# Layer-norm scales computed as a power on GpSimd, and two pieces of a first stage moved later

## The chip, the cores and the metric

The kernel runs on one core of one Trainium2 chip. A core has a matrix engine (TensorE, "PE"; its weight loads are listed as "PEld"), a vector engine (VectorE, "DVE"), a scalar engine with tabulated functions (ScalarE, "ACT"), a general engine (GpSimd, "POOL") and a queue engine that issues transfers (SyncE, "SP"). Matrix results land in eight banks of 128 x 512 float32. The metric is the device time of one execution in microseconds; a lower number is better.

## What is computed

Input `x` is 4 batches x 2048 rows x 256 columns, float32. Two layers follow each other, each a normalization whose result feeds two branches that are added to `x`:

```
def _layernorm(x, axis=-1, eps=1e-05):
    m = jnp.mean(x, axis=axis, keepdims=True)
    v = jnp.var(x, axis=axis, keepdims=True)
    return (x - m) / jnp.sqrt(v + eps)
...
    x = L0_attn_x
    xn = _layernorm(x, axis=-1)
    x = x + _L0_attn_ref(xn, ...) + _L0_ffn_ref(xn, ...)
    xn = _layernorm(x, axis=-1)
    x = x + _L1_attn_ref(xn, ...) + _L1_ffn_ref(xn, ...)
    return x
```

In layer 0, `_L0_attn_ref` is a gated linear recurrence along the rows (two 256 x 256 gate products, tanh, exp, a square root, then an associative scan). `_L0_ffn_ref` is attention with 16 heads of width 64, of which the 4 with the largest mean routing score are computed; softmax over all 2048 keys, then an output projection. In layer 1, `_L1_attn_ref` is causal attention with 16 heads of width 16, and `_L1_ffn_ref` a channel mix (mixing with the previous row, a squared ReLU, a sigmoid gate).

## The kernel before, in words

One Python function, `two_layers` (L73), writes all instructions. Batches are done one after the other. Inside a batch, layer 0 comes first and layer 1 second, and the tail of layer 1 is mixed with the head of the next batch. `in_order` (L26) ties the instructions of PE, DVE, ACT and POOL to the order in which the Python code emits them. So each engine works through its own list in that order, and an instruction that waits holds up everything behind it on its engine. The setup ahead of `in_order` is ordered by the tile scheduler. SP has its own list of transfers.

The order is written out by hand with generators. A stretch of work is a generator, each `yield` in it is a place to pause, and `steps(stream, count)` (L64) runs it on to its next pauses.

**The norm.** `Norm` (L243) holds a batch's rows `xt` in 16 tiles of 128 rows. `stats` (L253) puts mean and variance of a tile into `mv` (DVE). `root` (L257) takes Sqrt(variance + eps) on ACT, `inverse` (L261) the reciprocal on DVE; both work in place on `rs`. `rows` (L264) writes (x - mean) * rs into `xn` (DVE, one instruction a tile), and `turn` (L272) transposes four tiles of `xn` on PE and copies them into `xT`. The trace has a table load of ACT (ACT_TABLE_LOAD) ahead of each such Sqrt, and another ahead of the Exp or Tanh that follows it.

The norm of layer 1 is done in quarters of four tiles (`all_blocks`, L570, inside `attention0`). The norm of layer 0 of the next batch is done for all 16 tiles at once, in `prepared` (L994): it runs in the tail of layer 1, and for batch 0 at the very start of the kernel.

**The recurrence.** `recurrence` (L278) is a generator: 16 steps of `gates`, 9 steps of `chain` for the second half of the columns, then two steps of additions (L327: a constant is added to `y`, one 128 x 2048 instruction on DVE for each half `h`), then eight steps (L334 to L336) that each transpose a 128 x 512 block of `y` on PE and add it to `xt` on DVE. 26 of its 35 steps are done before `attention0` is entered, so the 26th, the addition for h = 0, is the last one ahead of it. The rest are its `background`.

**Attention of layer 0.** `attention0` (L562) goes over 4 heads x 8 pairs of row tiles, 32 pairs in all, plus two turns of its loop to drain (n = 0 to 33). A pair has an early tile `a` and a late tile `c`. Each tile needs scores (PE, four banks), four row maxima and their maximum `nm` (DVE, L499 and L503), four exponentials (ACT, L509), 16 transposes of the exponentials (PE, L517), four copies into `pT` (two on DVE, two on ACT, L523). `weigh` (L537) multiplies by the values, one loop turn later; `project` and `add` (L551, L557) follow two turns later. Banks are handed out in a ring of seven by `bank()` (L117), so a product that wants a bank waits until the bank's last content has been read.

In one turn the order is: first place for background, projections and norm (L606 to L608); transposes of the late tile of the pair before; second place (L621 to L623); projection, addition and, in the last eight pairs, `stats`; scores, maxima and exponentials of `a`; at n = 0 also the last four steps of `values0` (`rest_of_values`, L634); third place for the norm (L635); scores and exponentials of `c` and the weighing of the pair before; transposes of `a`; fourth place for the norm (L657).

A quarter of the norm takes eight such places, thus two pairs: nothing in two, then `root`, then `inverse` and `rows`, then one transposed half in each of two, then nothing in two. The quarters start at n = 27, 29, 31 and 33. At n = 33 there is no pair left to overlap with.

**Layer 1.** `opening1` (L725) sets up its projections. `Heads1.open` (L693) and `values1` (L704) fill tiles on POOL (L696, L711), and `layer1` (L806) uses POOL for masking (L791) and for adding partial results (L804). In the tail `steps(norming, 2)` (L917) runs the next batch's norm two steps at a time.

Of the kernel before, what the change touches and what calls it, by code (L numbers as in the profile page):

```python
# [10 lines left out]
FP = mybir.dt.float32  # L11
BF = mybir.dt.bfloat16
U32 = mybir.dt.uint32
AF = mybir.ActivationFunctionType
ALU = mybir.AluOpType
# [3 lines left out]
P = 128  # L19
QB = 512  # L20
EPS = 1e-5
# [42 lines left out]
def steps(stream, count):  # L64

    for _ in range(count):
        if next(stream, StopIteration) is StopIteration:
            return False
    return True
# [3 lines left out]
def two_layers(ctx: ExitStack, tc: tile.TileContext, x, Wa, Wx, ba, bx, Lam,  # L73
# [4 lines left out]
    PE, ACT, DVE, POOL, SP = nc.tensor, nc.scalar, nc.vector, nc.gpsimd, nc.sync  # L78
# [3 lines left out]
    NT = T // P  # L82
# [7 lines left out]
    const = ctx.enter_context(tc.tile_pool(name="const", bufs=1))  # L90
# [32 lines left out]
    def load_x(b):  # L123
        src = x[b].rearrange("(n p) d -> p n d", p=P)
        both = [half_tile(f"x_{b}_{i}").rearrange("p (n d) -> p n d", d=D) for i in range(2)]
        for q in range(NQ):
            SP.dma_start(rows_of(both, 4 * q, 4), src[:, 4 * q:4 * q + 4, :])
        return both

    def rows_of(both, n, count):  # L130
# [13 lines left out]
    POOL.memset(cmask, 0.0)  # L144
    POOL.affine_select(out=cmask[:, QB - P:QB], in_=cmask[:, QB - P:QB], compare_op=ALU.is_ge, fill=MASKED,
                       base=0, pattern=[[-1, P]], channel_multiplier=1)
    eps_c = const.tile([P, 1], FP, tag="eps", name="eps_c")
    POOL.memset(eps_c, EPS)
    quarter_c = const.tile([P, 1], FP, tag="quarter", name="quarter_c")
    POOL.memset(quarter_c, 0.25)  # L150
    heads_row = const.tile([P, NH], FP, tag="heads_row", name="heads_row")
# [91 lines left out]
    class Norm:  # L243
# [10 lines left out]
            DVE.bn_stats(self.st[:, t, :], rows_of(self.xt, t, 1)[:, 0, :])  # L254
            DVE.bn_aggr(self.mv[:, t, :], self.st[:, t, :])

        def root(self, t, n):  # L257
            ACT.activation(self.rs[:, t:t + n], self.mv[:, t:t + n, 1:2].rearrange("p n o -> p (n o)"),
                           AF.Sqrt, bias=eps_c)

        def inverse(self, t, n):  # L261
            DVE.reciprocal(self.rs[:, t:t + n], self.rs[:, t:t + n])

        def rows(self, q, i0, i1):  # L264
            if i0 == 0:
# [182 lines left out]
    def queries0(b, k, xT, ch, bank):  # L448

        qs = [half_tile(f"q0_{b}_{k + i}") for i in range(2)]  # L450

        def stream():
            for q in range(NQ):
                blk = slice(q * QB, (q + 1) * QB)
                ps = bank()
                for c in range(2):
                    PE.matmul(ps, lhsT=ch.wq[k // 2][:, c, :], rhs=xT[c][:, blk], start=(c == 0), stop=(c == 1))  # L457
                ACT.activation(qs[0][:, blk], ps, AF.Identity, bias=ch.bias_q[:, k // 2:k // 2 + 1])
                for i in range(2):
                    SP.dma_start(qs[1][i * DH:(i + 1) * DH, blk], qs[0][(1 - i) * DH:(2 - i) * DH, blk])  # L460
                yield
        return qs, stream()

    def keys0(b, k, xT, ch, bank):

        kT = c4.tile([P, HT], FP, tag="k0", name=f"k0_{b}_{k}", bufs=2)

        def stream():
            for j in range(NJ):
                ps = bank()  # L470
                for c in range(2):
                    for i in range(2):
                        k0 = i * HT + j * QB
                        PE.matmul(ps[i * DH:(i + 1) * DH, :], lhsT=ch.wk[k][:, c, :], rhs=xT[c][:, k0:k0 + QB],  # L474
                                  start=(c == 0), stop=(c == 1))
                ACT.activation(kT[:, j * QB:(j + 1) * QB], ps, AF.Identity, bias=ch.bias[:, 1, k:k + 1])
                yield
        return kT, stream()
# [83 lines left out]
    def attention0(b, xT, xt, ch, recurring, first, v, rest_of_values, norm, opening):  # L562


        NP = NT // 2
        qk, following = first, None
        background, projecting, norming = recurring, iter(()), iter(())
        older, before = None, None

        def all_blocks():  # L570


            for q in range(NQ):
                yield
                yield
                norm.root(4 * q, 4)
                yield
                norm.inverse(4 * q, 4)
                norm.rows(q, 0, 2)
                norm.rows(q, 2, 4)  # L580
                yield
                for c in range(2):
                    norm.turn(q, c, ACT.copy)
                    yield
                yield
                yield

        for n in range(NA * NP + 2):
            k, i = divmod(n, NP)
            if i == 0 and 0 < k < NA:  # L590
                steps(projecting, 100)
                qk = following
            new = Pair0(b, k, i, *qk, v, xt) if k < NA else None
            a, c = new.tiles if new else (None, None)
            if i == NP - 3 and k + 1 < NA:
                if k % 2:
                    qs, querying = queries0(b, k + 1, xT, ch, bank)
                else:
                    qs, querying = qk[0], iter(())
                kT, keying = keys0(b, k + 1, xT, ch, bank)  # L600
                following = qs, kT
                projecting = concat(querying, keying)
            if n == (NA - 1) * NP + 3:
                norming = all_blocks()

            steps(background, 1)  # L606
            steps(projecting, 1)
            steps(norming, 1)  # L608
            if n >= NA * NP:
                steps(opening, (2, 2)[n - NA * NP])  # L610
            if before:
                late = before.tiles[1]
                late.turn(1)
                late.turn(0)
                late.keep(1, 0, DVE.tensor_copy)
                late.keep(0, 0, DVE.tensor_copy)
                late.keep(0, 1, ACT.copy)
                late.keep(1, 1, ACT.copy)
                for tile_ in before.tiles:
                    tile_.share()  # L620
            steps(background, 1)  # L621
            steps(projecting, 1)
            steps(norming, 1)  # L623
            if older:
                older.project()
                older.add()
                if n - 2 >= (NA - 1) * NP:
                    for t in range(2):
                        norm.stats(2 * (n - 2 - (NA - 1) * NP) + t)
            if new:  # L630
                a.scores(0)
                a.scores(1)
                a.exponentials((0, 1))
                steps(rest_of_values, 4)  # L634
            steps(norming, 1)  # L635
            if new:
                c.scores(1)
            if n >= NA * NP:
                steps(opening, 1)
            if before:  # L640
                before.weigh(0)
            if new:
                c.scores(0)
                c.exponentials((1, 0))
            if before:
                before.weigh(1)
            if new:
                a.turn(1)
                a.turn(0)
                a.keep(1, 0, DVE.tensor_copy)  # L650
                a.keep(0, 0, DVE.tensor_copy)
                a.keep(1, 1, ACT.copy)
            if before:
                before.weighed()
            if new:
                a.keep(0, 1, ACT.copy)
            steps(norming, 1)  # L657
            older, before = before, new
        steps(background, 100)
        for _ in range(8):  # L660
            steps(norming, 1)
            steps(opening, 1)
        steps(norming, 100)
# [330 lines left out]
    def prepared(b, ready):  # L994

        xt = load_x(b)
        norm = Norm(xt, f"0_{b}", own_bank)
        ch = Chosen()
        ready.append((xt, norm.xT, ch))

        def go():
            for t in range(0, NT, 2):
                norm.stats(t)
                norm.stats(t + 1)
                yield
            norm.root(0, NT)
            yield
            norm.inverse(0, NT)
            for q in range(NQ):
                norm.rows(q, 0, 2)  # L1010
                yield
                norm.rows(q, 2, 4)
                yield
                yield
                for c in range(2):
                    norm.turn(q, c, DVE.tensor_copy)
                    yield
        return go(), choose(b, norm.xT, ch)
# [3 lines left out]
    with in_order(tc):  # L1022
# [3 lines left out]
        for b in range(B):  # L1026
# [20 lines left out]
            x1, norm = xt, Norm(xt, f"1_{b}", bank)  # L1047
# [36 lines left out]
```

## Time and profile before

| what | value |
|---|---|
| median of 3 runs (lowest, highest) | 4306.98 us (4306.27, 4307.82) |
| the profiled execution's own time | 4301.88 us |
| span of its trace | 4300.2 us |
| DVE busy | 3101.0 us (72%) |
| ACT busy | 2809.9 us (65%) |
| POOL busy | 1044.2 us (24%) |
| table loads ahead of a Sqrt of the norms (L258) | 20, 25.7 us |
| table loads ahead of the Exps of layer 0 (L509) | 16, 20.5 us |
| table loads ahead of the Exps of layer 1 (L788) | 7, 9.0 us |
| the norms' Sqrt (L258) | 20, 6.0 us |
| the norms' reciprocal (L262) | 20, 3.7 us |
| recurrence's additions (L327) | 8, 9.9 us |

The profile comes from one execution, recorded instruction by instruction. The span runs from its first to its last instruction; the execution's own time is 1.7 us more. Shares are of the span. A "group" is all instructions of one source line, engine and operation. "Idle before" is the time an engine stood still right before an instruction, and the name behind the arrow is what ended that idle time. An engine can be busy nearly all the time and still lose time in a few places, so the places where the busiest engine stood idle matter more than the shares.

### The profile page before, as it was taken

Reading aid. Unit: us, or ns where it says so; the run is one execution under the profiler, and the core shown is the slowest. Engines: PE = TensorE matmul, PEld = TensorE weight load, DVE = VectorE, ACT = ScalarE, POOL = GpSimd, SP = SyncE. Lnnn points to the kernel's source line nnn. Section 1 sums busy time; section 2 is a strip of 40 time slices with the busy share of each in tenths; the row PEclk is TensorE's granted clock in tenths of the full one; section 3 lists DMA queues with packets and bytes.
Section 4 is the critical chain, followed back from the end, with each engine's and each line's share of the span. In section 5 each row is a group of like instructions: output and inputs, shape, how many; then the busy total and the mean of one; then the engine's idle time right before and its main releaser. Section 6 shows DMA issues by size and latency. Waiting matters only on the chain.

```text
span 4300.2 us, 86329 instructions
## 1 busy us (share of the span) xinstructions
PE 4189.6 (97%) x32994; PEld 2345.5 (55%) x32994; DVE 3101.0 (72%) x7292; ACT 2809.9 (65%) x6388; POOL 1044.2 (24%) x1322
## 2 busy tenths in 40 slices
PE   6999999999999999999999999999999999999999
PEld 3777653334577764333457776433446766643334
DVE  5767678887577767888657775888856777588882
ACT  3666648886566664888656665588765666568884
POOL 0000015544100001554410000255440000036544
PEclk9999999999999999999999999999999999999999
DMA  3000010100100000010000000001000000100000
GB/s 85 1 11 2 6 17 17 18 25 17 26 1 11 1 9 16 17 37 6 19 24 1 11 1 18 6 17 37 7 19 23 1 11 1 21 5 17 16 7 23
DMA packets 70818, 65.79 MB, mean 15 GB/s; under 512 B 37234, under 2 KB 58628, under 8 KB 68868
## 3 DMA queue, kind: packets, MB, share of 16 engines
q1 hardware_dynamic: 66624, 57.19, 6.1%
q8 instruction: 260, 4.26, 0.4%
q10 hardware_dynamic: 3780, 3.07, 0.2%
q14 instruction: 154, 1.26, 0.1%
HBM read 16.70 MB, written 8.39 MB: 6 GB/s over the span
## 4 chain that ended last, share of the span: by engine, by line
PE 89%; DVE 5%; ACT 3%; issue 1%; POOL 1%; DMA 1%; ACTq 0%; SPq 0%; POOLq 0%; DVEq 0%
PE bank L786 15%; PE bank L761 14%; PE bank L797 12%; PE bank L517 10%; PE bank L495 10%; PE bank L542 10%; PE bank L972 4%; PE bank L291 3%; PE bank L688 3%; PE bank L555 2%; DVE mx L767 1%; PE bank L474 1%; PE bank L457 1%; PE bank L717 1%; PE bank L960 1%; ACT p L509 1%
## 5 line engine op out<-in xcount | busy, mean ns | idle before, releaser
L788 ACT ACTIVATE p<-bank 128x512 f32<-128x512 f32 (+3 forms) x2560 | 1183.1, 539 | 378.9 <-PE bank L786 275.1
L761 PE MATMUL bank<-k,q 32*128 32x512 f32 (+3 forms) x5120 | 1180.9, 584 | 2.2
L767 DVE TENSOR_REDUCE mx<-bank 128x1 f32<-128x512 f32 x1536 | 950.9, 683 | 197.2 <-PE bank L761 196.4
L786 PE MATMUL bank<-q,k 32*128 32x512 f32 (+3 forms) x5120 | 1074.0, 556 | 0.0
L509 ACT ACTIVATE p<-bank,nm 128x512 f32<-128x512 f32 x1024 | 690.4, 686 | 566.5 <-DVE nm L503 566.3
L804 POOL TENSOR_TENSOR o<-o,w 128x512 f32<-128x512 f32 (+3 forms) x576 | 627.0, 1088 | 796.0 <-ACT w L803 795.7
L786 PEld LDWEIGHTS bank<-q,k 32*128 32x128 f32 x5120 | 422.0, 184 | 544.6 <-ACT p L788 409.4
L499 DVE TENSOR_REDUCE mx<-bank 128x1 f32<-128x512 f32 x1024 | 645.9, 683 | 91.4 <-PE bank L495 90.6
L797 PE MATMUL bank<-p,v 128*17 128x512 f32 (+3 forms) x5120 | 601.3, 534 | 21.4 <-ACT p L788 14.3
L764 DVE CUSTOM_DVE_ANT_0 bank<-bank,cmask 128x128 f32<-128x128 f32 (+3 forms) x1024 | 473.1, 523 | 171.3 <-PE bank L761 116.4
L523 DVE COPY pT<-bank 128x512 f32<-128x512 f32 x512 | 353.1, 692 | 286.3 <-PE bank L517 267.9
L761 PEld LDWEIGHTS bank<-k,q 32*128 32x128 f32 x5120 | 473.5, 188 | 139.3 <-DVE mx L767 48.9
L542 PEld LDWEIGHTS bank<-pT,v 128*64 128x64 f32 x8192 | 442.0, 137 | 191.0 <-issue 191.0
L495 PE MATMUL bank<-k,q 64*128 64x512 f32 x2048 | 542.2, 609 | 0.9
L517 PE MATMUL bank<-ident,p 128*128 128x128 f32 x4096 | 490.8, 275 | 20.0 <-ACT p L509 19.8
L542 PE MATMUL bank<-pT,v 128*64 128x128 f32 x8192 | 502.8, 276 | 0.0
L517 PEld LDWEIGHTS bank<-ident,p 128*128 128x128 f32 x4096 | 445.1, 141 | 68.7 <-ACT p L509 29.8
L696 POOL MEMSET q<- 128x2048 f32 x16 | 28.9, 1808 | 1803.8 <-PE bank L542 1803.8
L803 ACT COPY w<-bank 128x512 f32<-128x512 f32 (+3 forms) x576 | 304.9, 529 | 107.2 <-PE bank L797 85.5
L523 ACT COPY pT<-bank 128x512 f32<-128x512 f32 x512 | 293.7, 601 | 55.6 <-PE bank L517 53.9
L797 PEld LDWEIGHTS bank<-p,v 128*17 128x17 f32 x5120 | 88.7, 95 | 439.8 <-ACT p L788 237.1
L495 PEld LDWEIGHTS bank<-k,q 64*128 64x128 f32 x2048 | 212.5, 188 | 170.0 <-issue 83.4
(164 smaller groups left out, 3346.7 us busy)
## 6 DMA issues: line engine op xcount, KB each, us to landing
x<-in_L_attn_x_dram SPq DMA_DIRECT2D x20, 512.0 KB
q<-q SPq DMA_DIRECT2D x64, 128.0 KB
vals<-o SPq DMA_DIRECT2D x256, 32.0 KB
out_dram<-x SPq DMA_DIRECT2D x32, 256.0 KB
q<-qp SPq DMA_DIRECT2D x48, 128.0 KB
k<-kp SPq DMA_DIRECT2D x48, 128.0 KB
q<-nmT SPq DMA_DIRECT2D x256, 2.0 KB
q<-qp SPq DMA_DIRECT2D x64, 32.0 KB
```

The source lines that it names most:

```text
L495: PE.matmul(self.s[j][i], lhsT=self.qT[i][half_, self.t * P:(self.t + 1) * P], rhs=self.kT[half_, j * QB:(j + 1) * QB], start=True, stop=True)
L499: DVE.tensor_reduce(self.mx[:, n:n + 1], self.s[j][i], AX.X, ALU.max)
L509: ACT.activation(self.p[j][:, i, :], self.s[j][i], AF.Exp, bias=nm, accum_out=self.sums[:, n:n + 1])
L517: PE.transpose(self.tr[j][i][:, n * P:(n + 1) * P], self.p[j][:, i, n * P:(n + 1) * P], ident)
L523: copy(self.pT[:, n0:n0 + 4, :], self.tr[j][i].rearrange("p (n q) -> p n q", q=P))
L542: PE.matmul(acc[i * DH:(i + 1) * DH, 0:P], lhsT=self.v[h][:, N * j + n, self.k * DH:(self.k + 1) * DH], rhs=tile_.pT[:, 8 * h + N * j + n, ...
L761: PE.matmul(s[:, 0:n], lhsT=self.qT[strip(h), self.qs], rhs=self.kT[strip(h), self.ks], start=True, stop=True)
L767: DVE.tensor_reduce(self.mx[:, h, :], s[:, 0:n], AX.X, ALU.max)
L786: PE.matmul(s[:, c0:QB], lhsT=self.kT[strip(h), self.ks], rhs=self.qT[strip(h), self.q0 + c0:self.q0 + QB], start=True, stop=True)
L788: ACT.activation(p[:, h % 2, c0:QB], s[:, c0:QB], AF.Exp, scale=SC1)
L797: PE.matmul(acc[32 * h:32 * h + DH1 + 1, c0:QB], lhsT=self.v[h], rhs=self.p[h // 2][:, h % 2, c0:QB], start=True, stop=True)
L804: POOL.tensor_tensor(self.o[:, c0:QB], self.o[:, c0:QB], w[:, c0:QB], ALU.add)
```

## The change

Three things are changed.

1. `root` is gone. `inverse` now adds eps on DVE (one instruction) and raises the result to the power -0.5 on POOL, against a constant tile `minus_half` of 128 x 16. In `all_blocks` it is called at the place where `root` was called; the place behind it holds `rows` alone. In `prepared` it also takes the place of `root`.
2. At n = 0 the two `background` steps are left out. The addition for h = 1 then falls on the first place of n = 1, and the eight transposed blocks on n = 1 to 5 (one, two, two, two, one) instead of n = 0 to 4 (one, two, two, two, one).
3. Of the last four steps of `values0`, two stay behind the exponentials of the first `a`, and two go behind the scores and exponentials of the first `c`.

```diff
@@ -144,8 +144,8 @@
     POOL.memset(cmask, 0.0)
     POOL.affine_select(out=cmask[:, QB - P:QB], in_=cmask[:, QB - P:QB], compare_op=ALU.is_ge, fill=MASKED,
                        base=0, pattern=[[-1, P]], channel_multiplier=1)
-    eps_c = const.tile([P, 1], FP, tag="eps", name="eps_c")
-    POOL.memset(eps_c, EPS)
+    minus_half = const.tile([P, NT], FP, tag="minus_half", name="minus_half")
+    POOL.memset(minus_half, -0.5)
     quarter_c = const.tile([P, 1], FP, tag="quarter", name="quarter_c")
     POOL.memset(quarter_c, 0.25)
     heads_row = const.tile([P, NH], FP, tag="heads_row", name="heads_row")
@@ -254,12 +254,10 @@
             DVE.bn_stats(self.st[:, t, :], rows_of(self.xt, t, 1)[:, 0, :])
             DVE.bn_aggr(self.mv[:, t, :], self.st[:, t, :])
 
-        def root(self, t, n):
-            ACT.activation(self.rs[:, t:t + n], self.mv[:, t:t + n, 1:2].rearrange("p n o -> p (n o)"),
-                           AF.Sqrt, bias=eps_c)
-
         def inverse(self, t, n):
-            DVE.reciprocal(self.rs[:, t:t + n], self.rs[:, t:t + n])
+            rs = self.rs[:, t:t + n]
+            DVE.tensor_scalar(rs, self.mv[:, t:t + n, 1:2].rearrange("p n o -> p (n o)"), EPS, None, ALU.add)
+            POOL.tensor_tensor(rs, rs, minus_half[:, 0:n], ALU.pow)
 
         def rows(self, q, i0, i1):
             if i0 == 0:
@@ -573,9 +571,8 @@
             for q in range(NQ):
                 yield
                 yield
-                norm.root(4 * q, 4)
-                yield
                 norm.inverse(4 * q, 4)
+                yield
                 norm.rows(q, 0, 2)
                 norm.rows(q, 2, 4)
                 yield
@@ -603,7 +600,8 @@
             if n == (NA - 1) * NP + 3:
                 norming = all_blocks()
 
-            steps(background, 1)
+            if n:
+                steps(background, 1)
             steps(projecting, 1)
             steps(norming, 1)
             if n >= NA * NP:
@@ -618,7 +616,8 @@
                 late.keep(1, 1, ACT.copy)
                 for tile_ in before.tiles:
                     tile_.share()
-            steps(background, 1)
+            if n:
+                steps(background, 1)
             steps(projecting, 1)
             steps(norming, 1)
             if older:
@@ -631,7 +630,7 @@
                 a.scores(0)
                 a.scores(1)
                 a.exponentials((0, 1))
-                steps(rest_of_values, 4)
+                steps(rest_of_values, 2)
             steps(norming, 1)
             if new:
                 c.scores(1)
@@ -644,6 +643,7 @@
                 c.exponentials((1, 0))
             if before:
                 before.weigh(1)
+            steps(rest_of_values, 2)
             if new:
                 a.turn(1)
                 a.turn(0)
@@ -1003,9 +1003,8 @@
                 norm.stats(t)
                 norm.stats(t + 1)
                 yield
-            norm.root(0, NT)
+            norm.inverse(0, NT)
             yield
-            norm.inverse(0, NT)
             for q in range(NQ):
                 norm.rows(q, 0, 2)
                 yield
```

The order of instructions that follows from it: on ACT, 58 table loads become 19, and the 20 Sqrt instructions of the norms are gone. On DVE the count stays the same, an addition in place of each reciprocal. POOL has 20 more instructions: 16 of 128 x 4 and 4 of 128 x 16. In each batch the first three powers of layer 1's norm stand in POOL's list ahead of the two fills of `Heads1.open(0, ...)`, and the fourth stands behind these and ahead of the fills of the values (L711) and of `Heads1.open(1, ...)`.

More of the change, by code (lines that the diff above doesn't have):

```diff
@@ L575, in all_blocks @@
                 yield
-                norm.root(4 * q, 4)
+                norm.inverse(4 * q, 4)
                 yield
-                norm.inverse(4 * q, 4)
                 norm.rows(q, 0, 2)
```

## The prediction

> **What bounds the kernel now.** I read the page's busy times and its chain first, then the waits of PE, then the order of time around the places that the waits name.
>
> ```profile
> PE 4189.6 (97%) x32994; PEld 2345.5 (55%) x32994; DVE 3101.0 (72%) x7292; ACT 2809.9 (65%) x6388; POOL 1044.2 (24%) x1322
> PE 89%; DVE 5%; ACT 3%; issue 1%; POOL 1%; DMA 1%; ACTq 0%; SPq 0%; POOLq 0%; DVEq 0%
> ```
>
> PE sets the time: it is busy for 4189.6 of 4300.2 us, and the chain that ended last is 89% PE. Work taken from ACT, DVE or POOL is worth only what PE waits for it. So the waits of PE (total, times, longest) hold nearly all there is to win:
>
> ```profile
> PE bank L517 <- ACT p L509: 19.8, 16, 1.3
> PE bank L334 <- DVE y L327: 18.9, 4, 4.7
> PE bank L275 <- DVE xn L269: 9.9, 11, 2.1
> ```
>
> The first row is 16 waits of some 1.24 us: four at n = 0 (one a batch) and twelve at the roots of n = 27, 29 and 31. The second is one wait of 4.73 us a batch at n = 0. Of the third, 4 x 1.12 us belong to the root of n = 33, and the rest to the start. Together 19.8 + 18.9 + 4.5 = 43.2 us, 1.0% of the span. Batch 1 in order of time (start, duration, instruction, idle before it):
>
> ```profile
> 1159.30 2.47 DVE L327 TENSOR_SCALAR y<-y,added 128x2048 f32<-128x2048 f32 x2
> 1160.72 0.87 PE L334 MATMUL bank<-ident,y 128*128 128x128 f32 x4 [4.73 <-DVE y L327]
> 1161.53 3.38 PE L495 MATMUL bank<-k,q 64*128 64x512 f32 x8
> 1163.63 2.60 DVE L499 TENSOR_REDUCE mx<-bank 128x1 f32<-128x512 f32 x4 [1.26 <-PE bank L495]
> 1166.27 0.16 DVE L503 TENSOR_REDUCE nm<-mx 128x1 f32<-128x4 f32 x1
> 1176.65 0.66 PE L517 MATMUL bank<-ident,p 128*128 128x128 f32 x4 [1.25 <-ACT p L509]
> ```
>
> PE stands at L334 until the first addition ends, and the second addition and L336 stand on DVE ahead of the first maxima. The idle time also costs clock. In the windows view, whose third column from the right is the granted clock, that stretch reads
>
> ```profile
> 1160.70:1165.00 4.30, 4.28 (x13) 1.83 (x14) 3.02 (x5) 0.00 (x0) 0.00 (x0) 0.60 0.01 4
> ```
>
> so 0.60, and 1.00 in the windows before and after. The eight score products there take 3.38 us, and eight at full clock 1.99 (L495 at 1171.94). A root, and what follows it:
>
> ```profile
> 1518.37 1.28 ACT L258 ACT_TABLE_LOAD   x1
> 1519.67 0.30 ACT L258 ACTIVATE rs<-mv,eps_c 128x4 f32<-128x4 f32 x1
> 1519.98 1.28 ACT L509 ACT_TABLE_LOAD   x1
> ...
> 1521.28 0.69 ACT L509 ACTIVATE p<-bank,nm 128x512 f32<-128x512 f32 x1
> 1521.60 0.17 DVE L262 RECIPROCAL rs<-rs 128x4 f32<-128x4 f32 x1
> 1521.80 1.38 DVE L269 TENSOR_SCALAR xn<-x,mv,rs 128x256 f32<-128x256 f32 x4
> ...
> 1522.11 0.66 PE L517 MATMUL bank<-ident,p 128*128 128x128 f32 x4 [1.23 <-ACT p L509]
> ...
> 1523.45 2.20 PE L517 MATMUL bank<-ident,p 128*128 128x128 f32 x16
> ```
>
> The root holds c's exponentials from 1518.37 to 1521.28, 2.91 us. The last four transposes of `a` want the bank that the first of them reads, and wait 1.23 us. But close behind, PE needs `xn`, which DVE has only from 1521.80 on.
>
> **Part by part. The first pair (the two moves).** After the change DVE goes from the first addition (1159.30 + 1.28 = 1160.6) straight to the maxima: 2.60 us, so nm at 1163.1 instead of 1166.27, 3.2 us earlier. The exponentials of `a`, 0.66 us apart, free its banks at about 1163.9, 1164.6, 1165.2 and 1165.9. PE, done with the values at 1156.0, does a's scores (1.99) and two value steps (half of the 7.17 us that L443 takes for four): 1161.6. c's second score product then waits for a bank until 1163.9: the stall goes there, some 1.5 us of it, too short to judge whether it costs clock. c's scores end at about 1165.9, its nm follows at 1166.7, its exponentials at 1166.9 to 1169.6. The other two value steps keep PE at work from 1165.9 to 1169.5, and then the transposes of `a` find their fourth bank freed at 1168.9, so the 1.25 us are gone too. They end at 1171.4 instead of 1177.3. On DVE, n = 1 then has two copies to 1171.7, the second addition (1.28, which runs while PE is at the late tile's 1.9 us of transposes), two copies, the shares (0.6) and L336 (0.68): 1175.4, where the next maxima began at 1181.71 before. Gain 6.3 us. Against it, the last blocks come later: pairs with two blocks, one and none last 12.79, 12.39 and 11.82 us (distances of the L503 rows), so one block more at n = 4 and one at n = 5 cost 0.4 + 0.6 = 1.0. Net 5.3 a batch, 21.2 for four. Bounds: if only DVE's 3.2 us come through, 3.2 - 1.0 = 2.2 a batch, 8.8; if all three things seen at n = 0 vanish, 4.73 + 1.39 + 1.25 = 7.4, 29.5.
>
> **The twelve roots inside pairs.** ACT loses 1.28 + 0.30 + 1.28 us, and c's exponentials start 2.9 us earlier. PE still cannot go on much earlier: the copies on DVE end at 1521.68 as before, `rows` start where the reciprocal did, at 1521.60, 0.20 earlier. At the root of n = 33, where nothing else holds PE, the step from `rows` (1599.68) to the work behind the transposes (1601.28) is 1.60; so the late tile starts at 1523.20 instead of 1523.45. Its 16 transposes then need 1.86 (32 take 3.71 in a pair without a root) instead of the 2.03 to the next PE row. Gain 0.25 + 0.17 = 0.42, 12 x 0.42 = 5.0. What is late next is DVE's `rows`. Bounds: 0.20 a root if nothing but the reciprocal goes (2.4), 1.23 + 0.35 if the whole wait and the slow transposes go (19). The added addition of eps, priced as the reciprocal's 0.17, stands ahead of c's last maximum, where DVE idles 0.29 for PE.
>
> On a switch of tables the trace has 1.28 us and an ACTIVATE 0.02 us behind its end. [...]
>
> **The price of a power.** No row shows one. From below, the two-input adds of L804 take 0.455, 0.725, 1.002 and 1.269 us for 128, 256, 384 and 512 columns, a line of 0.18 us plus 2.1 ns a column: 0.19 us for 4 columns, 0.22 for 16. From above, the dearest POOL row, L696 with 1.81 us, and four times that, 7.2, for 16 columns. The nearest row is the narrowest two-input one, 0.455, so I take 0.45 for 4 columns and 1.8 for 16.
>
> **Where it has cover.** At n = 27, 29 and 31 the power starts soon after 1515.4 and `rows` at 1521.60: 6 us of cover. Behind the third of them on POOL stand the two L696 fills (3.6 us), which ran at 1548 before and now come at about 1574; their transfers on SP start at 1583.67. In `prepared` DVE already stands 1.91 us for the Sqrt; a power behind POOL's L962 (ending 2092.55) has 4.9 us before POOL's next work at 2097.49, and DVE idles 4.64 us before L982. ACT's saved 2.9 us there are worth nothing, since PE runs without a gap from 2088.81 to 2102. At the start of the kernel the power lies between about 27.9 and 31.1, where DVE waits for L215 and PE: 3.2 us of cover, and 0.4 us won from the reciprocal. Without cover stands the root of n = 33:
>
> ```profile
> 1599.13 0.30 ACT L258 ACTIVATE rs<-mv,eps_c 128x4 f32<-128x4 f32 x1 [0.63 <-DVE mv L255]
> 1599.68 1.38 DVE L269 TENSOR_SCALAR xn<-x,mv,rs 128x256 f32<-128x256 f32 x4
> 1600.15 1.30 PE L275 MATMUL bank<-ident,xn 128*128 128x128 f32 x4 [1.12 <-DVE xn L269]
> ```
>
> From the last mean and variance (1599.10) to `rows` are 0.58 us; with eps (0.17), the power (0.45) and three handovers (0.04 each, as from Sqrt to reciprocal) 0.74. So 0.2 lost, 0.7 for four; between -0.4 and +6.1 (1.81 us each). Behind it on POOL come the fills of the values and of the next strips, 4.2 us, done by 1604; the strips' transfers come after 1616.
>
> [...]
>
> **The sum.** -21.2 - 5.0 + 0.7 - 0.4 = -25.9 us: span 4300.2 to 4274.3. The profiled execution (4301.88) is 5.1 us under the median, so the same difference on the median gives 4306.98 - 25.9 = 4281.1.
>
> **Rivals.** *The waits change place.* The new wait of c's scores at n = 0 grows and `rows` hold the roots: only the low bounds come, -8.8 - 2.4 + 0.7 - 0.4 = -10.9, 4296. For it: both sides of n = 0 lean on the same DVE list. Against it: PE's two value steps now lie where it would wait. *All of PE's idle time goes:* the 43.2 us of the three waits, 4264. Against it: `rows` start only 0.2 earlier. *The power is dear:* if POOL takes its columns or values one at a time, with 3.6 us for 4 columns (twice the dearest row) and 14.5 for 16, the roots of n = 33 lose 4 x 3.3 = 13, the three in `prepared` 3 x 9.6 = 29 (DVE and POOL both stand behind them), the start 11: +53 on the -26.6 of the rest, 4333, slower. It decides from about 2.2 us for 4 columns on (8 + 12 + 6 = 26). For it: no row shows POOL at anything but single additions, products and fills. Against it: none of POOL's 1322 instructions takes more than 1.82 us.
>
> **How the numbers follow.** Forecast 0.62, waits change place 0.18, all idle time 0.08, dear power 0.12. A measurement here can tell about 0.2% (8.6 us) from no change. Faster: 0.62 + 0.08 and 0.14 of the second case; no change 0.04; slower 0.12. The likeliest, 4281, is predicted; its own range is 4268 to 4293. The range 4262 to 4299 takes in the second and third case and leaves out the dear power and a little at each end.
>
> **What would show it.** Right: no wait at L332 (the old L334) for an addition, nm of the first pair 3 us sooner, pairs with a root at 15.4 us between L503 rows instead of 15.79, 19 table loads, powers under 1 us. Wrong: a power of over 2 us, PE waiting for `xn` at n = 33 longer than 1.3 us, or a new PE wait of over 3 us behind c's scores at n = 0.

## The result and the profile after

| kernel | median | lowest, highest | runs |
|---|---|---|---|
| before | 4306.34 us | 4305.02, 4307.97 | 12 |
| after | 4307.98 us | 4302.38, 4311.35 | 12 |

The ratio, taken over all runs, is 1.0001, with a 95% interval of 0.9992 to 1.001: no change that can be measured. 4281 was predicted, with a range that ended at 4299. The profiled execution of after took 4303.30 us, its span is 4301.6. Both profiled executions lie some 4.5 us below the median of their kernel.

From the page of after: the busy times, the chain by engine, and the group of the new powers (busy us, mean ns | idle before):

```profile
PE 4198.0 (98%) x32994; PEld 2353.7 (55%) x32994; DVE 3113.8 (72%) x7292; ACT 2758.2 (64%) x6329; POOL 1072.9 (25%) x1342
...
PE 87%; DVE 5%; issue 5%; ACT 1%; POOL 1%; DMA 1%; ACTq 0%; SPq 0%; POOLq 0%; DVEq 0%
...
L260 POOL TENSOR_TENSOR rs<-rs,minus_half 128x4 f32<-128x4 f32 (+1 forms) x20 | 27.9, 1394 | 1891.1 <-DVE rs L259 1867.1
```

ACT shed 51.7 us, and its share of the chain went from 3% to 1%. But PE is *busier* by 8.4 us and DVE by 12.8 with the same number of instructions: something runs slower. The waits of PE (total us, times, longest) show where to look:

```profile
PE bank L273 <- DVE xn L267: 36.8, 25, 5.5
PE bank L493 <- ACT p L507: 5.7, 4, 1.4
```

The 18.9 us for the addition and the 19.8 us for the exponentials are gone. In their place the wait for the norm's rows has grown from 9.9 to 36.8 us. Two places of batch 1 in order of time (start, duration, instruction, idle before it). First n = 0:

```profile
1159.34 1.28 DVE L325 TENSOR_SCALAR y<-y,added 128x2048 f32<-128x2048 f32 x1
1160.54 2.48 DVE L497 TENSOR_REDUCE mx<-bank 128x1 f32<-128x512 f32 x4
1163.05 0.16 DVE L501 TENSOR_REDUCE nm<-mx 128x1 f32<-128x4 f32 x1
1164.07 2.46 PE L493 MATMUL bank<-k,q 64*128 64x512 f32 x6 [1.42 <-ACT p L507]
```

The first `nm` comes at 1163.05 instead of 1166.27; 1163.1 was forecast. c's scores wait 1.42 us for a bank; some 1.5 was forecast. Then n = 33, where the last quarter of the norm is made:

```profile
1592.39 0.17 DVE L259 TENSOR_SCALAR rs<-mv 128x4 f32<-128x4 f32 x1
...
1592.65 1.01 POOL L260 TENSOR_TENSOR rs<-rs,minus_half 128x4 f32<-128x4 f32 x1 [21.56 <-DVE rs L259]
1593.60 0.54 POOL L711 MEMSET v<- 128x112 f32 x3
1593.69 4.83 DVE L267 TENSOR_SCALAR xn<-x,mv,rs 128x256 f32<-128x256 f32 x4 [1.12 <-POOL rs L260]
1594.00 1.85 POOL L696 MEMSET q<- 128x2048 f32 x1
...
1595.79 1.95 POOL L696 MEMSET k<- 128x2048 f32 x1
...
1596.05 0.33 PE L273 MATMUL bank<-ident,xn 128*128 128x128 f32 x1 [3.76 <-DVE xn L267]
...
1597.93 1.11 PE L273 MATMUL bank<-ident,xn 128*128 128x128 f32 x3 [1.56 <-DVE xn L267]
...
1598.84 3.62 PE L717 MATMUL bank<-wv,xT 128*128 128x256 f32 x8
```

The four `rows` take 4.83 us instead of 1.38, and they do so while POOL fills. PE waits 3.76 + 1.56 us instead of 1.12. Behind it the eight products of L717 take 3.62 us; in the kernel before they took 1.89. There the two long fills of POOL ended at 1596.31, 3.4 us ahead of the `rows`; PE released them, and DVE stood idle for 7.87 us meanwhile:

```profile
1592.77 1.80 POOL L696 MEMSET q<- 128x2048 f32 x1 [15.36 <-PE bank L542]
...
1594.51 1.80 POOL L696 MEMSET k<- 128x2048 f32 x1
...
1597.15 0.88 DVE L560 SCALAR_TENSOR_TENSOR x<-bank,rc,x 128x256 f32<-128x256 f32 x2 [7.87 <-PE bank L555]
...
1601.28 1.89 PE L717 MATMUL bank<-wv,xT 128*128 128x256 f32 x8
```

The windows of the stretch in after (window, length, busy us of PE, PEld, DVE, ACT and POOL, granted clock, DMA share, GB/s):

```profile
1592.00:1597.20 5.20, 0.62 (x2) 0.14 (x1) 4.01 (x5) 0.69 (x1) 4.55 (x6) 1.00 0.23 52
1597.20:1604.00 6.80, 6.07 (x18) 4.79 (x19) 1.32 (x3) 1.82 (x4) 0.54 (x1) 0.50 0.01 4
```

So the clock is halved for the 6.8 us after the wait. By the `nm` of the last early tile (n = 31) a batch of after is on average 6.4 us ahead of one of before. From there to the first scores of layer 1 (PE, L761) it takes 52.7 to 53.05 us instead of 46.41, that is 6.3 to 6.6 more, and the lead is gone in each of the four batches, to within 0.8 us.

### The profile page after: what moved, and what is told of

Read it like the earlier page. It is cut to its first block, busy times and chain, and to the rows that moved or that the text cites. A ratio compares the mean times of both kernels' runs of the same rounds, so it can differ in the third digit from the quotient of the medians.

```text
span 4301.6 us, 86306 instructions
## 1 busy us (share of the span) xinstructions
PE 4198.0 (98%) x32994; PEld 2353.7 (55%) x32994; DVE 3113.8 (72%) x7292; ACT 2758.2 (64%) x6329; POOL 1072.9 (25%) x1342
## 4 chain that ended last, share of the span: by engine, by line
PE 87%; DVE 5%; issue 5%; ACT 1%; POOL 1%; DMA 1%; ACTq 0%; SPq 0%; POOLq 0%; DVEq 0%
PE bank L786 15%; PE bank L761 14%; PE bank L797 12%; PE bank L493 10%; PE bank L515 10%; PE bank L540 10%; PE bank L972 4%; PE bank L289 3%; PE bank L688 2%; PE bank L553 2%; PE bank L717 1%; DVE mx L767 1%; PE bank L472 1%; PE bank L455 1%; PE bank L960 1%
## 5 line engine op out<-in xcount | busy, mean ns | idle before, releaser
L761 PE MATMUL bank<-k,q 32*128 32x512 f32 (+3 forms) x5120 | 1180.5, 580 | 2.2
L497 DVE TENSOR_REDUCE mx<-bank 128x1 f32<-128x512 f32 x1024 | 646.6, 683 | 85.5 <-PE bank L493 85.2
L761 PEld LDWEIGHTS bank<-k,q 32*128 32x128 f32 x5120 | 470.2, 187 | 143.0 <-DVE mx L767 50.2
L260 POOL TENSOR_TENSOR rs<-rs,minus_half 128x4 f32<-128x4 f32 (+1 forms) x20 | 27.9, 1394 | 1891.1 <-DVE rs L259 1867.1
```

Of the source, the lines that this page charges most:

```text
L497: DVE.tensor_reduce(self.mx[:, n:n + 1], self.s[j][i], AX.X, ALU.max)
L761: PE.matmul(s[:, 0:n], lhsT=self.qT[strip(h), self.qs], rhs=self.kT[strip(h), self.ks], start=True, stop=True)
```

## The experiments

My theory: the fills beside `rows` are the loss. In the kernel before the two long ones ran while DVE was idle. Now all of them stand behind the fourth power in POOL's list, and the power releases them at the very moment at which it releases `rows`. The rivals: the power's own duration (1.01 us, where 0.45 was priced); POOL instead of ACT in the chain of the last quarter, whatever runs beside it; fills that come late and hurt layer 1; and the moves at n = 0. `held` below is a new 128 x 1 tile; a copy into it reads what POOL shall wait for. The numbers "last early `nm` to layer 1" are distances between rows of the traces, from the `nm` of the last early tile to the first scores of layer 1, one value for each kind of batch where they differ. The root of n = 31 lies in this stretch too.

| kernel | median | ratio to before (95%) | last early `nm` to layer 1 |
|---|---|---|---|
| e1, fills behind rows | 4290.68 | 0.9965 (0.9951 to 0.9978) | 46.81, 48.49 |
| e2, Sqrt for the last quarter | 4288.76 | 0.9958 (0.9944 to 0.9971) | 46.06 |
| e3, before with the fills beside rows | 4329.18 | 1.0053 (1.0038 to 1.0069) | 52.2 to 52.55 |
| e7, only the values' fills beside | 4291.06 | 0.9965 (0.9951 to 0.9979) | 46.99, 48.67 |
| e4, moves alone | 4290.47 | 0.9962 (0.9949 to 0.9976) | 46.42 |
| e5, power alone | 4328.64 | 1.0052 (1.0038 to 1.0066) | 51.6 to 53.0 |
| e6, a product for the power | 4306.47 | 0.9998 (0.9988 to 1.0007) | 51.0 to 51.55 |
| e8, Sqrt for the last quarter, values three and one | 4276.52 | 0.9933 (0.9919 to 0.9947) | 46.06 |

The first four stand against a kernel before of 4305.69 us (9 runs), the last four against one of 4307.0 (15 runs).

**e1: the fills behind the rows.** After, and POOL waits for the last row ahead of the fills. By my theory `rows` would come back to about 1.4 us, PE's wait to about 1.9 us, and the time to 4308 - 4 x 5.7 = 4285 us, with no half clock at n = 33.

```diff
                 norm.rows(q, 2, 4)
+                if q == NQ - 1:
+                    POOL.tensor_copy(held, norm.xn[:, 3, D - 1:D])
```

> The changed kernel, but on POOL a copy of one column of the last row tile's xn stands between the fourth power and the fills (L711, L696), so the fills run after the rows of n = 33 instead of beside them. [...] Rival 'the power itself' (1.01 us and its handovers on the path): nothing changes, 4308. Rival 'late fills hurt layer 1': slower than 4308, since the fills come later still.

The same place in order of time, with the power still there:

```profile
1594.24 1.38 DVE L268 TENSOR_SCALAR xn<-x,mv,rs 128x256 f32<-128x256 f32 x4 [1.12 <-POOL rs L261]
...
1594.71 1.30 PE L274 MATMUL bank<-ident,xn 128*128 128x128 f32 x4 [1.87 <-DVE xn L268]
...
1595.69 0.19 POOL L580 COPY held<-xn 128x1 f32<-128x1 f32 x1 [1.48 <-PE bank L274]
...
1595.81 0.54 POOL L714 MEMSET v<- 128x112 f32 x3
1595.85 1.89 PE L720 MATMUL bank<-wv,xT 128*128 128x256 f32 x8
```

`rows` are back at 1.38 us, the products at 1.89, and 17 us of the median come back. The wait that is left, 1.87 instead of 1.12, is what the power costs here; where 48.49 us were measured (batches 0 and 3), the clock was halved for 3.4 us as well, which was not expected. The fills come still later here than in after and POOL is still in the chain, so neither of these makes the loss.

**e2: Sqrt for the last quarter.** After, with the old root and reciprocal for q = 3 only; the fills then run ahead of the quarter again. I expected about 4282 us by my theory, the same if the power itself is the cause, and less than 4308 if late fills are.

```diff
-                norm.inverse(4 * q, 4)
+                if q == NQ - 1:
+                    norm.root(4 * q, 4)
+                else:
+                    norm.inverse(4 * q, 4)
                 yield
+                if q == NQ - 1:
+                    norm.reciprocal(4 * q, 4)
```

> The changed kernel, but the norm's last quarter (n = 33) takes Sqrt on ACT and the reciprocal on DVE as before, so POOL's fills wait for nothing there. [...] Two table loads a batch come back, hidden (ACT idles there).

46.06 us: the whole loss of n = 33 is gone. The 0.35 us less than in before (46.41) go to the root of n = 31, which is still a power here; the moves alone change nothing in this stretch (46.42, e4). But e1 and e2 both missed their expected times by some 6 us on the slow side. In e1 the half clock at n = 33 is a part of it (1.7 us in each of two batches). In both kernels time is lost at n = 0, in some batches only. A window of e1 in batch 0, and under it the same one of after:

```profile
103.00:110.00 7.00, 7.00 (x16) 4.43 (x16) 2.23 (x4) 5.02 (x14) 0.00 (x0) 0.51 0.00 0
```

```profile
103.00:110.00 7.00, 7.00 (x37) 5.30 (x36) 3.52 (x7) 5.67 (x16) 0.00 (x0) 1.00 0.00 0
```

PE shows busy for all 7.00 us of both, but at a clock of 0.51 against 1.00, and 16 instructions came through against 37 (not all of one size). From the first `nm` to that of the last early tile such a batch takes 406.2 to 406.6 us instead of 403.1 to 403.7. The profiled run of e1 has it in batches 0 and 3, that of e2 in all four (in batch 1 for 3.4 us, not 6.8, and there it takes 405.2), that of after in none.

**e3: the kernel before, with the fills beside the rows.** If the theory holds, the loss must appear without any power. POOL is made to wait for the Sqrt. I expected `rows` of 4 to 5 us and 4324 to 4332 us; if late fills hurt layer 1, a slower kernel with `rows` at 1.4 us.

```diff
                 norm.root(4 * q, 4)
+                if q == NQ - 1:
+                    POOL.tensor_copy(held, norm.rs[:, NT - 1:NT])
```

> The kernel before, Sqrt and reciprocal in place, no power; only a copy of one column of rs on POOL behind the last quarter's Sqrt, which holds the fills back until then. [...] 'The power itself': 4306, no change. [...]

```profile
1606.39 0.18 POOL L579 COPY held<-rs 128x1 f32<-128x1 f32 x1 [33.70 <-ACT rs L259]
1606.51 0.54 POOL L714 MEMSET v<- 128x112 f32 x3
1606.83 4.79 DVE L270 TENSOR_SCALAR xn<-x,mv,rs 128x256 f32<-128x256 f32 x4
1606.91 1.85 POOL L699 MEMSET q<- 128x2048 f32 x1
...
1608.70 1.80 POOL L699 MEMSET k<- 128x2048 f32 x1
...
1610.71 1.44 PE L276 MATMUL bank<-ident,xn 128*128 128x128 f32 x4 [4.78 <-DVE xn L270]
...
1611.94 3.62 PE L720 MATMUL bank<-wv,xT 128*128 128x256 f32 x8
```

Slower by 23 us, with the same signs: `rows` at 4.79, PE waiting 4.78, the products at 3.62. This settles that the fills bring the loss without any power. It also splits it: a batch loses 5.8 to 6.1 us here, of which 4.78 - 1.12 = 3.7 are the longer wait and 2.1 to 2.4 the clock behind it.

**e7: only the small fills beside the rows.** After, with POOL held ahead of the second set of strips. By my theory only the 0.8 us of small fills would hold the first row: a wait of PE of about 2.7 us, full clock behind it, 4288 to 4290 us.

```diff
+        POOL.tensor_copy(held, heads.norm.xn[:, 3, D - 1:D])
         ...
             heads.open(1, i)
```

> The changed kernel, but the copy that waits for the rows stands behind the three value fills (L711, 0.8 us) and ahead of the two strip fills (L696, 3.6 us). [...] 'The power itself': 4308.

```profile
1594.96 0.54 POOL L712 MEMSET v<- 128x112 f32 x3
1595.05 1.56 DVE L268 TENSOR_SCALAR xn<-x,mv,rs 128x256 f32<-128x256 f32 x4 [1.12 <-POOL rs L261]
...
1595.70 1.29 PE L274 MATMUL bank<-ident,xn 128*128 128x128 f32 x4 [2.06 <-DVE xn L268]
```

The three fills of L711 cost `rows` 0.18 us, and the median is e1's. So the two long fills of `open(1, ...)`, 3.6 us, make the loss. PE's wait came out shorter than expected, 2.06 us instead of 2.7, and yet the clock was halved for 3.4 us at n = 33 in batches 0 and 2 (the 48.67 us), against the expectation.

**e6: a product for the power.** `ALU.pow` becomes `ALU.mult`, all else as in after; the kernel then leaves out the power, so its norms have another scale. By my theory only the power's own 0.8 us a batch would go: 4305 us, with `rows` still at 4 us and more.

```diff
-            POOL.tensor_tensor(rs, rs, minus_half[:, 0:n], ALU.pow)
+            POOL.tensor_tensor(rs, rs, minus_half[:, 0:n], ALU.mult)
```

> The changed kernel with a product on POOL in place of the power (the norms' scale is then wrong, all instructions else are the same). The product should take 0.2 us or so instead of 1.01 us. [...] 'The power itself': the loss at n = 33 goes, about 4285 us.

```profile
1598.99 0.20 POOL L260 TENSOR_TENSOR rs<-rs,minus_half 128x4 f32<-128x4 f32 x1 [22.39 <-DVE rs L259]
...
1599.23 5.00 DVE L267 TENSOR_SCALAR xn<-x,mv,rs 128x256 f32<-128x256 f32 x4 [0.32 <-POOL rs L260]
```

POOL's instruction takes 0.20 us instead of 1.01, `rows` still take 5.00, and the time stays where after's is. The last stretch is 1.5 to 1.9 us shorter than after's and still 4.6 to 5.1 us longer than before's. So the power's duration, with the clock behind it, is about a quarter of the loss there, and the fills are the rest. The median shows little even of that quarter, as the clock that is lost at n = 0 differs from run to run: in the profiled run of e6, its slowest, three of the four batches have it.

**e4 and e5: the parts alone.** e4 is the kernel before with the two moves of n = 0; e5 is after with these undone. I expected 4288 us of e4 (up to 4300 where the clock halves at n = 0) and 4325 of e5.

```diff
@@ e4, on before @@
-            steps(background, 1)
+            if n:
+                steps(background, 1)
 ...
-                steps(rest_of_values, 4)
+                steps(rest_of_values, 2)
 ...
+            steps(rest_of_values, 2)
@@ e5, on after @@
-            if n:
-                steps(background, 1)
+            steps(background, 1)
 ...
-                steps(rest_of_values, 2)
+                steps(rest_of_values, 4)
 ...
-            steps(rest_of_values, 2)
```

> The kernel before with the two moves at n = 0 alone (background a pair later, values two and two); Sqrt and reciprocal as before. [...] Rival 'the gain of the moves is an illusion, lost again by the end of layer 0': 4306.

> The changed kernel without the two moves: power on POOL, background and values as before. [...] Rival 'the power pays and the moves eat it': below 4300.

Waits of PE, e4 first, then e5:

```profile
PE bank L517 <- ACT p L509: 14.8, 12, 1.2
...
PE bank L495 <- ACT p L509: 5.7, 4, 1.4
```

```profile
PE bank L273 <- DVE xn L267: 37.1, 23, 5.5
...
PE bank L332 <- DVE y L325: 18.9, 4, 4.7
```

The moves alone win 16.5 us, the power alone loses 21.6. Their sum, +5.1, stands near after's +1.6, with after's runs spread over 9 us: no sign that the parts touch each other much. e4 keeps the twelve waits of 1.24 us at the roots and has no wait for the addition; e5 has it the other way round, and with it the long wait for `rows`.

**e8: three steps and one.** e2, and of the last four steps of `values0` three stay behind a's exponentials and one goes behind c's. PE then has more to do where c's scores wait for their bank.

```diff
-                steps(rest_of_values, 2)
+                steps(rest_of_values, 3)
 ...
-            steps(rest_of_values, 2)
+            steps(rest_of_values, 1)
```

> The kernel with Sqrt in the last quarter, and three of the four value steps behind the first a's exponentials, one behind c's (instead of two and two). If the 1.4 us wait and the slow pace of c's scores at n = 0 are what halves the clock there: wait shorter than 1 us, no half clock, the transposes of a 1.5 us sooner, total 4289 - 4 x (1.5 to 4.6) = 4270 to 4283 us. If the clock falls anyway: 4283 to 4289.

In order of time, at n = 0 of batch 1, then the window of batch 0 that was slow in e1:

```profile
1158.12 3.13 PE L502 MATMUL bank<-k,q 64*128 64x512 f32 x8 [0.74 <-ACT p L516]
```

```profile
103.00:110.00 7.00, 7.00 (x44) 5.26 (x42) 5.66 (x9) 5.68 (x16) 0.00 (x0) 1.00 0.00 0
```

The wait is halved to 0.74 us, none of the four batches has a slow window at n = 0, and from the first `nm` to that of the last early tile it takes 402.2 to 402.6 us in each. 4276.52 us, 30 less than before (0.9933), and its five runs lie between 4276.3 and 4278.4. This version beats both kernels.

## Why the prediction was wrong, point by point

**What failed: the cover at n = 33.** The step was the sentence "Behind it on POOL come the fills of the values and of the next strips, 4.2 us, done by 1604; the strips' transfers come after 1616." The fills were held against those who need their content, and these are indeed in no hurry. They were not held against what runs at the same time: a fill that waits for the power starts with the `rows` that wait for the power. Term by term, four times +0.2 us were in the sum; measured were 6.3 to 6.6 each, 25 to 26 in all, which is the whole forecast gain (25.9). e3 shows the mechanism without the power, e1, e2 and e7 show that the time comes back when the long fills stand elsewhere, and e6 that the power's length is the smaller part. The prediction's own sign for this came true: it would be wrong if PE waited for `xn` at n = 33 longer than 1.3 us, and PE waited 5.3 to 5.5 us. In after's trace POOL had stood idle for 21.56 us ahead of the power. In e2, where no power holds them, the fills ran at 1585.46 to 1589.02, so there was room for them ahead of it. The prediction's reading that the two fills of the first strips "ran at 1548 before" holds for one of them; the other ran at 1563.98.

**The dear power** was the rival on the slow side. Its point of decision, 2.2 us for 4 columns, wasn't reached: 1.01 us for 4 columns and 2.91 to 2.99 for 16, against the 0.45 and 1.8 that I took from POOL's adds. Within the bounds, but over twice the chosen value for the small one. At n = 33 it costs 1.87 - 1.12 = 0.75 us of PE's wait (e1), where 0.2 were forecast. The three powers in `prepared` and the one at the start are covered, as forecast; the one at the start, the first of all, takes 2.99 us.

**The first pair** went as forecast up to the clock: `nm` to a tenth of a microsecond, c's wait 1.42 for 1.5, no wait for the addition, and the next pair's `nm` at 1178.23 (15.18 later; 17.96 before). The new wait I had called "too short to judge whether it costs clock". It does in some batches of some runs, about 3 us each (e1, e2), and in none of the four batches of the trace with a wait of 0.74 us (e8). The moves alone brought 16.5 us (e4), where 21.2 stood in the sum. In the profiled run of e4 one batch of four, batch 0, has the halved clock at n = 0; its pairs take 407.3 us instead of 404.2 to 404.5. In that run this is 3 of the missing 4.7 us. In the trace of after no batch has it, and the lead by n = 31, some 25.6 us in four batches, is near what the sum had for the moves and eight roots (21.2 + 3.4). That is in part luck: the order of n = 0 is the same in e2 and e6, and there four and three batches lose clock.

**The twelve roots.** Those of n = 27 and 29 brought 0.55 us each (15.24 us between `nm` rows instead of 15.79), not 0.42. Behind the root of n = 31 there is no further pair; e2 shows 0.35 us there (46.06 instead of 46.41). Together that is 5.8 us, where 5.0 were forecast.

**Waits change place** was priced at 4296, as a wait at n = 0 or at the roots. The wait that did change place was a third, at n = 33, which no rival named.

## What to carry to other kernels

When a step moves to another engine's queue, list what stands behind it in that queue and ask what it will now run beside, not only who needs its result. Put independent fills ahead of an instruction that waits, or behind the consumer of its result, not between them. A stall that is moved rather than removed can cost more by the clock behind it than by its length: at n = 0 a wait of 1.42 us cost some 3 us more where the clock was halved, and one of 0.74 us cost none in the trace of e8.

## What the runs showed of the hardware

**A long POOL fill holds DVE's `rows`.** In after at n = 31 the fills and the `rows` lie one after the other (start, duration):

```profile
1567.54 1.80 POOL L696 MEMSET q<- 128x2048 f32 x1
...
1569.28 1.81 POOL L696 MEMSET k<- 128x2048 f32 x1
```

```profile
1572.54 1.38 DVE L267 TENSOR_SCALAR xn<-x,mv,rs 128x256 f32<-128x256 f32 x4
```

There four rows take 1.38 us. Beside the fills single rows of 0.41 us take 2.30 and 1.97 (batches 1 and 2) or one takes 4.06 (0 and 3): each waits until a fill, or both, have ended (in batch 1 the two rows end at 1595.99 and 1597.88, the fills at 1595.85 and 1597.74). The maxima, which read the banks of the matrix results, lose nothing: in after's trace 12 of those of L497 meet a long fill and last 0.68 us on average, as the other 1012 do. The fills themselves are hardly slower, 1.85 and 1.95 us. So here it is the row that loses, by what is left of the fills; why the rows wait and the maxima do not, no run shows.

**A power's time** on POOL grows with its columns: 1.01 us for 4 and 2.91 to 2.99 for 16, some 0.16 us a column between these two. A product of the same shapes takes 0.20 and 0.30. The line gives the count, the shortest, median and longest time in ns, the first and last start, and the shapes:

```profile
L260 POOL TENSOR_TENSOR rs<-rs,minus_half x20: 1007/1008/2988, 27.0 to 3715.9; 128x4 f32<-128x4 f32 x16, 128x16 f32<-128x16 f32 x4
```

**The clock** fell to one half for 6.8 us behind waits of 3.76 + 1.56 us (after, batch 1), and behind 1.42 us in some batches only. The same order of instructions at n = 0 has it in different batches of different runs, and after's runs spread over 9 us. The traces show what goes with it. In all ten of them the granted clock changes only at multiples of one step of 3.41 us, and every stretch at half clock but the last, which the end of the trace cuts short, is one to four steps long (3.41 to 13.65 us in before, 6.83 or 13.65 in after). The wait of 1.42 us stands in 24 batches (after, e1, e2, e4, e6, e7). In the ten batches where at least 1.40 us of it lie within one step, the clock is halved for the next two steps. Where a border splits the wait (1.36 us or less in one step), 13 batches keep the full clock and one (e2, batch 1) loses it for one step. So it seems to be chance, the wait's place among the steps, that decides; no run was made to test this.
